# A spiking recommender on one core: the padding row is taken out by a matrix product instead of by masks

## The chip, the cores and the metric

The kernel runs on one core of one Trainium2 chip. The metric is the device time of one execution in microseconds (us); lower is better. Before the change it is 1647.34 us, the median of three runs.

## The reference

For 1024 sequences of 50 items the reference looks up a row of 128 values for each item in a table of 100001 rows, forms a running mean, normalizes it over the batch, drives a leaky spiking neuron with it, and multiplies the mean spike of each sequence with the whole table. Row 0 of the table stands for padding and counts as zero.

```python
emb = emb_table.at[0].set(0.0)                    # 100001 x 128
e = emb[seq]                                      # 1024 x 50 x 128
prefix = jnp.cumsum(e, axis=1)
denom = jnp.minimum(t_idx[None, :], lengths[:, None])   # t_idx = 1..50
uF = prefix / denom[:, :, None]
mean, var = uF.mean(axis=0), uF.var(axis=0)       # over the batch
y = (uF - mean) * lax.rsqrt(var + BN_EPS) * gamma + beta
def step(v, x):                                   # x: y of one time step
    v = v + (x - v) / TAU                         # TAU = 2
    spike = (v - V_TH >= 0)                       # V_TH = 1
    return v - spike * V_TH, spike
_, spikes = lax.scan(step, v0, x_seq)
scores = spikes.mean(axis=0) @ emb.T              # 1024 x 100001, float32
```

The result is 409.6 MB.

## The kernel before

The kernel has two parts with a seam. The order of all instructions on each engine is the order of the program text (`tc.manual_schedule()`): nothing is reordered by a planner. Tiles with the same tag share a place, and an instruction that writes a tile waits for the last readers of what lay there.

**First part: 50 steps, one for each position t.** The layout is transposed: 128 features on the partitions, the 1024 sequences in the free dimension. For each step GpSimd issues 8 indirect DMAs (`gather`, L204), each of which brings the table rows of 128 sequences into one 128x128 piece of the tile `e`. The tile has two buffers. `gather(t + 2)` stands inside step t, and its first DMA has to wait until TensorE has read `e` of step t. `idx` holds the item numbers; the first two tiles are gathered ahead of the loop.

The table's row 0 isn't zero in memory. ScalarE therefore multiplies each gathered piece by `some`, which is 1 where the index is above 0 and 0 elsewhere (`masked`, L249): 8 instructions a step, four ahead of `over` (L254) and four behind it, at the end of step t for the tile of step t + 1.

TensorE transposes the 8 pieces (L296) and adds them into two PSUM tiles `pre[0]` and `pre[1]`, one for each half of the batch, which thereby hold the running sum. Ahead of the loop a product of zeros (L275) opens the two sums. For each half, VectorE divides by the length or the step (`uF`, L307) and takes the statistics (`bs`, L308). Then, for the whole step: the aggregate (`mv`, L312), the square root on ScalarE (`r`, L316), the centring of `uF` on ScalarE (L323), on VectorE the rest of the potential after the spike (`rest`, which writes `negv`, L258), a reciprocal and three tiny operations for the scale `a` (L329 to L342), the input `x` on ScalarE into the tile of `v` (L346), the count of the spikes of the step before (`spiked`, L261), and the new potential `v` (`step`, L349). ScalarE then writes `d`, which is v minus the threshold (`over`, L254). `rest` needs `d`. `v` lies in two PSUM tiles, `v0` and `v1`, by turns.

In two late steps (t = 42 and 44) the first two 1024-item tiles of the table are prepared for the second part (`prepare`): 8 transposes (L135) into a PSUM tile `pt`, a copy, and a subtraction (L152), so that a tile is held as a high and a low part.

The last step is split. Its potential is made in three pieces of the batch: `pieceA` (128 sequences), `pieceB` (512) and `pieceC` (384), so that the products for the first 128 sequences can begin before the others are done. `near` holds what the first piece needs of the old potential, and `vA` and `countA` finish that piece. `keep_busy` (L270) issues transposes whose result nobody reads, 12 between the last real ones and 16 on `near` ahead of the first products.

**Second part: the products.** For each tile of 1024 items and each of the 8 blocks of 128 sequences TensorE multiplies the counts with the high and the low part (L159), VectorE (L476) and ScalarE (L478) by turns scale the result out of PSUM, and SP stores it.

**Setup.** SP loads `idx`, `len_i`, `gb` (gamma and beta), and then the first tiles of the table (`rows`); VectorE computes `some` (L216), the reciprocal lengths `rl`, their broadcast `rb` (L221), and `rlen` after 8 transposes of `rb` (L224), and clears `negv` (L240) and `count`. `rb` and every `uF` share one place.

The pieces of the code that the prediction follows:

Of the kernel before, what the change touches and what calls it, by code (L numbers as in the profile page):

```python
# [12 lines left out]
F32 = mybir.dt.float32  # L13
BF16 = mybir.dt.bfloat16
F32R = mybir.dt.float32r
I32 = mybir.dt.int32
U32 = mybir.dt.uint32
AF = mybir.ActivationFunctionType
ALU = mybir.AluOpType

P = 128
BN_EPS = 1e-5
V_TH = 1.0
HALF = 1024
KQ = HALF // P
BANK = 512
GROUP = 6
AHEAD = 6
TWICE = 2
ASIDE = 2  # L30
SHIFT = TWICE + ASIDE
# [7 lines left out]
def rec_kernel(  # L39
# [9 lines left out]
    nc = tc.nc  # L49
    B, T = seq.shape  # L50
    N, D = table.shape
# [119 lines left out]
    with ExitStack() as ph:  # L171
# [9 lines left out]
        nc.sync.dma_start(out=idx, in_=seq.rearrange("(p n) t -> p n t", n=NB))  # L181
        len_i = once.tile([P, NB], I32, tag="len_i", name="len_i")
        nc.sync.dma_start(out=len_i, in_=lengths.rearrange("(p n) -> p n", n=NB))
        gb = once.tile([P, 2], F32, tag="gb", name="gb")
        nc.sync.dma_start(out=gb[:, 0:1], in_=gamma.rearrange("(d o) -> d o", o=1))
        nc.sync.dma_start(out=gb[:, 1:2], in_=beta.rearrange("(d o) -> d o", o=1))
# [14 lines left out]
        def gather(t):  # L201
            es[t] = gp.tile([P, B], F32, tag="e", name=f"e_{t}")
            for n in range(NB):
                nc.gpsimd.indirect_dma_start(  # L204
                    out=es[t][:, n * P : (n + 1) * P],
                    out_offset=None,
                    in_=table,
                    in_offset=bass.IndirectOffsetOnAxis(ap=idx[:, n, t : t + 1].bitcast(U32), axis=0),
                )

        make_identity(nc, ident)
        rb = up.tile([P, NB, P], F32, tag="uF", name="rb")
        gather(0)

        some = once.tile([P, NB, T], F32, tag="some", name="some")
        nc.vector.tensor_single_scalar(some, idx, 0.0, ALU.is_gt)  # L216

        rl = once.tile([P, NB], F32, tag="rl", name="rl")
        nc.vector.tensor_copy(rl, len_i)
# [7 lines left out]

        hgb = once.tile([P, 3], F32, tag="hgb", name="hgb")
        nc.vector.tensor_scalar_mul(hgb[:, 0:1], gb[:, 0:1], 0.25)
        nc.vector.tensor_scalar_mul(hgb[:, 2:3], gb[:, 0:1], -0.25)  # L230
        nc.vector.tensor_scalar_mul(hgb[:, 1:2], gb[:, 1:2], 0.5)
        eps = once.tile([P, 1], F32, tag="eps", name="eps")
        nc.vector.memset(eps, BN_EPS)
        less = once.tile([P, 1], F32, tag="less", name="less")
# [7 lines left out]

        pre = [accp.tile([P, BANK], F32, tag=f"pre{h}", name=f"pre{h}") for h in range(B // BANK)]

        def masked(t, ns):

            for n in ns:
                part = es[t][:, n * P : (n + 1) * P]
                nc.scalar.activation(part, part, AF.Identity, scale=some[:, n, t : t + 1])  # L249

        def over(t, v):

            d = lp.tile([P, B], BF16, tag="d", name=f"d_{t}")
            nc.scalar.activation(d, v, AF.Identity, bias=less)  # L254
            return d

        def rest(d, v, cs):
            nc.vector.scalar_tensor_tensor(negv[:, cs], d[:, cs], 0.0, v[:, cs], ALU.is_ge, ALU.subtract)  # L258

        def spiked(out, cs, v):  # L260
            nc.vector.scalar_tensor_tensor(out, v, V_TH, count[:, cs], ALU.is_ge, ALU.add)  # L261
# [9 lines left out]

        v = None

        for h in range(B // BANK):
            nc.tensor.matmul(  # L275
                pre[h],
                lhsT=count[:, :P],
                rhs=count[:, h * BANK : (h + 1) * BANK],
                start=True,
                stop=False,  # L280
                skip_group_check=True,
            )
        masked(0, range(NB))
        gather(1)
        for t in range(T):
            last = t == T - 1
            e = es.pop(t)
            if last:
                rest(d, v, pieceA)
                near = once.tile([P, P], F32, tag="r0", name="near")  # L290
                nc.vector.tensor_scalar(near, negv[:, :P], -0.5, hgb[:, 1:2], ALU.mult, ALU.add)
            uF = up.tile([P, B], F32, tag="uF", name=f"uF_{t}")
            bs = sp.tile([P, B // BANK, 6], F32, tag="bs", name=f"bs_{t}")
            for h, cs in enumerate(halves):
                for k in range(0, BANK, P):
                    nc.tensor.matmul(  # L296
                        pre[h][:, k : k + P],
                        lhsT=e[:, h * BANK + k : h * BANK + k + P],
                        rhs=ident,
                        start=False,  # L300
                        stop=last,
                        is_transpose=True,
                        skip_group_check=True,
                    )
                    if last and h and k + P < BANK:
                        keep_busy(ident, KQ // 2)
                nc.vector.scalar_tensor_tensor(uF[:, cs], rlen[:, cs], 1.0 / (t + 1), pre[h], ALU.max, ALU.mult)  # L307
                nc.vector.bn_stats(bs[:, h, :], uF[:, cs])  # L308
            if t + 2 < T:
                gather(t + 2)  # L310
            mv = sp.tile([P, 2], F32, tag="mv", name=f"mv_{t}")
            nc.vector.bn_aggr(mv, bs.rearrange("p h s -> p (h s)"))  # L312


            r = sp.tile([P, 1], F32, tag="r", name=f"r_{t}")
            nc.scalar.activation(r, mv[:, 1:2], AF.Sqrt, bias=eps)  # L316
            if last:
                centred = once.tile([P, P], F32, tag="r0hi", name="centred")
                nc.vector.tensor_scalar(centred, uF[:, :P], mv[:, 0:1], hgb[:, 2:3], ALU.subtract, ALU.mult)
                w = sp.tile([P, 1], F32, tag="w", name="w")  # L320
                nc.vector.tensor_scalar_add(w, mv[:, 1:2], BN_EPS)
            else:
                nc.scalar.activation(uF, uF, AF.Identity, bias=mv[:, 0:1], scale=-1.0)  # L323


            if t and not last:
                rest(d, v, whole)

            nc.vector.reciprocal(r, r)  # L329
            q = sp.tile([P, 1], F32, tag="q", name=f"q_{t}")  # L330
            a = sp.tile([P, 1], F32, tag="a", name=f"a_{t}")
            if last:
                nc.vector.tensor_scalar(q, w, r, r, ALU.mult, ALU.mult)
                nc.vector.scalar_tensor_tensor(q, q, 3.0, r, ALU.subtract, ALU.mult)
                vA = once.tile([P, P], F32, tag="r0n", name="vA")
                nc.vector.scalar_tensor_tensor(vA, centred, q, near, ALU.mult, ALU.add)
                spiked(countA, slice(0, P), vA)
                nc.vector.tensor_mul(a, q, hgb[:, 0:1])
            else:
                nc.vector.scalar_tensor_tensor(q, mv[:, 1:2], BN_EPS, r, ALU.add, ALU.mult)  # L340
                nc.vector.tensor_scalar(q, q, r, 3.0, ALU.mult, ALU.subtract)
                nc.vector.tensor_scalar(a, q, r, hgb[:, 0:1], ALU.mult, ALU.mult)  # L342


            def x(vt, cs):
                nc.scalar.activation(vt, uF[:, cs], AF.Identity, bias=hgb[:, 1:2], scale=a)  # L346

            def step(vt, cs):
                nc.vector.scalar_tensor_tensor(vt, negv[:, cs], -0.5, vt, ALU.mult, ALU.add)  # L349

            if not last:
                vt = vp.tile([P, B], F32, tag=f"v{t % 2}", name=f"v_{t}")
                x(vt, whole)
                if t:
                    spiked(count, whole, v)
                step(vt, whole)
                v = vt
                if t == T - 2:
                    spiked(count, whole, v)
                masked(t + 1, range(NB // 2))  # L360
                d = over(t, v)
                if t in (T - 8, T - 6):
                    q = (t - T + 8) // 2
                    pair(q)
                    prepare(q, vp.tile([P, HALF], F32, tag="v1", name=f"pt_{q}"))
                    if q == TWICE - 1:
                        for k in range(TWICE):
                            rows[GROUP + ASIDE + k] = first[:, k, :]
                        nc.sync.dma_start(
                            out=first[:, :TWICE, :],  # L370
                            in_=table[(GROUP + ASIDE) * HALF : (GROUP + SHIFT) * HALF, :].rearrange(
                                "(q p k) d -> p q (k d)", p=P, k=KQ
                            ),
                        )

                masked(t + 1, range(NB // 2, NB))


        keep_busy(near, 2 * KQ)
# [1 line left out]
            nc.scalar.activation(uF[:, cs], uF[:, cs], AF.Identity, bias=mv[:, 0:1], scale=-1.0)  # L381

        po0 = accp.tile([P, HALF], F32, tag="po0", name="po_0_0")
        po1 = vp.tile([P, HALF], F32, tag="v1", name="po_0_1")
        o0 = gp.tile([P, HALF], F32, tag="e", name="o_0_0")
        o1 = gp.tile([P, HALF], F32, tag="e", name="o_0_1")
        firsts = [(q, po, o, h, cs) for q, po, o in ((0, po0, o0), (1, po1, o1)) for h, cs in enumerate(halves)]
# [14 lines left out]
        rest(d, v, pieceC)  # L402
        for f in firsts:
            first_store(*f)
        vC = vp.tile([P, B - BANK - P], F32, tag="v0", name="vC")
        x(vC, pieceC)
        step(vC, pieceC)
        spiked(countC, pieceC, vC)
# [109 lines left out]
```

## Time and profile before

| | before |
|---|---|
| three runs | 1647.17, 1647.34, 1648.22 us |
| median | 1647.34 us |
| the profiled execution: own time | 1647.17 us |
| its span in the profile | 1645.4 us |
| granted TensorE clock, mean | 0.96 |
| first part, to the last step's square root | 583.5 us |
| from there to the end | 1061.9 us |
| busy in the span: TensorE, VectorE, ScalarE, GpSimd | 63%, 57%, 48%, 23% |
| DMA engines in the second part | 98% busy |

The span runs from the first to the last instruction that the profiler recorded; the execution's own time is 1.77 us longer. Busy shares are means over two parts with different limits: GpSimd, for instance, is busy only while the steps run, at about 0.7 of the time, and idle afterwards. In a row of a timeline the columns are the start, the duration, the engine, the line of the program, the operation, and in brackets the idle time of that engine just before, with what ended it. A group's row gives the busy time and the mean of one instruction in ns, then the idle time ahead of the group's instructions and what ended most of it.

### The profile page before, as it was taken

How to read it: one execution, taken by the hardware profiler on the slowest of the kernel's cores; microseconds unless marked ns; L12 is line 12 of the kernel's file. 1: busy time of each engine (PE TensorE's matmuls, PEld its weight loads, DVE VectorE, ACT ScalarE, POOL GpSimd, SP SyncE). 2: the span in 40 equal slices, each digit the busy share in tenths (PEclk: the TensorE clock that was granted, in tenths of full speed). 3: DMA queues.
4: the chain of work that ended last, by engine and by line, in shares of the span. 5: the costliest groups of instructions: out<-in, count | busy, mean ns of one | idle time of the engine just before them, and what ended most of it. 6: DMA issues, size and time to landing. Idle time of an engine off the chain costs nothing.

```text
span 1645.4 us, 12553 instructions
## 1 busy us (share of the span) xinstructions
PE 1034.7 (63%) x4358; PEld 778.3 (47%) x4358; DVE 945.4 (57%) x1112; ACT 791.6 (48%) x1095; POOL 379.4 (23%) x406
## 2 busy tenths in 40 slices
PE   3222222222222289889998888888888888788884
PEld 1111111111111177667776666666666666666663
DVE  4656666666665765666655555555545555455642
ACT  4455555554554555555644444444444444444442
POOL 7666666666666500000000000000000000000000
PEclk9999999999999999999998999899999999999998
DMA  9611111111111169999999999999999999999998
GB/s 354 227 46 45 46 46 47 50 46 46 49 45 59 50 279 413 409 421 412 404 428 429 429 424 423 416 432 417 408 430 425 427 422 406 430 423 419 426 401 356
DMA packets 51171, 488.06 MB, mean 297 GB/s; under 512 B 10063, under 2 KB 10192, under 8 KB 29860
## 3 DMA queue, kind: packets, MB, share of 16 engines
q1 hardware_dynamic: 30608, 430.80, 62.2%
q0 software_dynamic: 12800, 26.24, 5.4%
q10 hardware_dynamic: 7700, 30.23, 4.5%
q8 instruction: 34, 0.56, 0.1%
q14 instruction: 29, 0.24, 0.0%
HBM read 77.62 MB, written 409.60 MB: 296 GB/s over the span
## 4 chain that ended last, share of the span: by engine, by line
DMA 42%; DVE 17%; PE 17%; ACT 10%; issue 7%; another core or an unknown queue 6%; POOL 0%; ACTq 0%; SPq 0%; DVEq 0%
DMA scores<-o 41%; PE po L159 13%; PE pre L296 3%; DVE bs L308 3%; DVE o L476 3%; DVE uF L307 3%; ACT o L478 3%; DVE negv L258 2%; ACT e L249 2%; ACT d L254 2%; DVE v L349 2%; ACT v L346 1%; ACT uF L323 1%; DVE pairs L152 1%
## 5 line engine op out<-in xcount | busy, mean ns | idle before, releaser
L476 DVE TENSOR_SCALAR o<-po 128x1024 f32<-128x1024 f32 (+1 forms) x391 | 467.8, 1214 | 324.7 <-DMA scores<-o 177.7
L478 ACT ACTIVATE o<-po 128x1024 f32<-128x1024 f32 x391 | 392.2, 1026 | 499.2 <-DMA scores<-o 352.6
L204 POOL DMA_INDIRECT e<-in_L_rec_emb_table,idx x400 | 378.7, 947 | 187.5 <-issue 107.7
L296 PE MATMUL pre<-ident,e 128*128 128x128 f32 x400 | 138.4, 474 | 412.0 <-ACT e L249 208.2
L159 PE MATMUL po<-pairs,countB 128*128 128x512 f32 (+1 forms) x1120 | 291.4, 407 | 57.4 <-ACT o L478 57.4
L296 PEld LDWEIGHTS pre<-ident,e 128*128 128x128 f32 x400 | 73.3, 183 | 477.0 <-ACT e L249 224.1
L159 PE MATMUL po<-pairs,countC 128*128 128x512 f32 (+1 forms) x840 | 239.0, 431 | 56.5 <-ACT o L478 49.0
L159 PEld LDWEIGHTS po<-pairs,countB 128*128 128x128 f32 x1120 | 211.4, 194 | 117.8 <-ACT o L478 75.2
L159 PEld LDWEIGHTS po<-pairs,countC 128*128 128x128 f32 x840 | 167.7, 207 | 108.5 <-ACT o L478 61.1
L307 DVE SCALAR_TENSOR_TENSOR uF<-rlen,pre 128x512 f32<-128x512 f32 x100 | 68.7, 687 | 186.4 <-remote 95.9
L152 DVE TENSOR_TENSOR pairs<-pt,pairs 128x1024 fp32r<-128x1024 f32 x70 | 85.3, 1218 | 95.3 <-ACT pairs L151 95.2
L249 ACT ACTIVATE e<-e,some 128x128 f32<-128x128 f32 x400 | 127.3, 388 | 6.3 <-DMA e<-in_L_rec_emb_table,idx 6.1
L316 ACT ACTIVATE r<-mv,eps 128x1 f32<-128x1 f32 x50 | 14.7, 295 | 222.2 <-DVE mv L312 122.4
L135 PE MATMUL pt<-ident,rows 128*128 128x128 f32 (+1 forms) x768 | 105.2, 282 | 18.1 <-issue 11.5
L135 PEld LDWEIGHTS pt<-ident,rows 128*128 128x128 f32 (+1 forms) x768 | 94.9, 148 | 35.2 <-issue 18.8
L159 PE MATMUL po<-hi,countB 128*128 128x512 f32 x208 | 85.7, 412 | 12.5 <-ACT o L478 12.2
L151 ACT CAST pairs<-pt 128x1024 fp32r<-128x1024 f32 x70 | 70.1, 1013 | 41.5 <-PE pt L135 41.5
L159 PE MATMUL po<-lo,countB 128*128 128x512 f32 x208 | 83.5, 401 | 0.0
L159 PE MATMUL po<-hi,countC 128*128 128x512 f32 x156 | 68.5, 439 | 16.2 <-ACT o L478 15.2
L346 ACT ACTIVATE v<-uF,hgb,a 128x1024 f32<-128x1024 f32 x49 | 59.2, 1207 | 30.9 <-DVE a L342 15.3
L308 DVE BATCH_NORM_STATS2 bs<-uF 128x6 f32<-128x512 f32 x100 | 69.4, 694 | 3.4
L159 PE MATMUL po<-pairs,countA 128*128 128x512 f32 x280 | 68.6, 394 | 4.0 <-ACT o L478 3.4
(79 smaller groups left out, 795.0 us busy)
## 6 DMA issues: line engine op xcount, KB each, us to landing
scores<-o SPq DMA_DIRECT2D x96, 3072.0 KB
scores<-o SPq DMA_DIRECT2D x32, 1536.0 KB
scores<-o SPq DMA_DIRECT2D x30, 1024.0 KB
rows<-in_L_rec_emb_table ACTq DMA_DIRECT2D x19, 1536.0 KB
scores<-o SPq DMA_DIRECT2D x8, 2896.5 KB
rows<-in_L_rec_emb_table SPq DMA_DIRECT2D x5, 3072.0 KB
e<-in_L_rec_emb_table,idx POOLq DMA_INDIRECT x400
rows<-in_L_rec_emb_table SPq DMA_DIRECT2D x2, 1024.0 KB
```

The lines of the kernel that those rows point to most:

```text
L135: nc.tensor.transpose(pt[:, k0 : k0 + pw], r[:pw, k0 : k0 + D], ident[:pw, :pw])
L151: nc.scalar.copy(vh, vp)
L152: nc.vector.tensor_tensor(vl, vp, vh.bitcast(F32), ALU.subtract)
L159: nc.tensor.matmul(po[:, :kw], lhsT=counts[n], rhs=part[:, k0 : k0 + kw], start=j == 0, stop=j == 1,)
L204: nc.gpsimd.indirect_dma_start(out=es[t][:, n * P : (n + 1) * P], out_offset=None, in_=table, in_offset=bass.IndirectOffsetOnAxis(ap=idx[: ...
L249: nc.scalar.activation(part, part, AF.Identity, scale=some[:, n, t : t + 1])
L296: nc.tensor.matmul(pre[h][:, k : k + P], lhsT=e[:, h * BANK + k : h * BANK + k + P], rhs=ident, start=False, stop=last, is_transpose=True, ...
L307: nc.vector.scalar_tensor_tensor(uF[:, cs], rlen[:, cs], 1.0 / (t + 1), pre[h], ALU.max, ALU.mult)
L308: nc.vector.bn_stats(bs[:, h, :], uF[:, cs])
L346: nc.scalar.activation(vt, uF[:, cs], AF.Identity, bias=hgb[:, 1:2], scale=a)
L476: nc.vector.tensor_scalar_mul(o[:, h0 : h0 + hw], po[:, :hw], 1.0 / T)
L478: nc.scalar.mul(o[:, h0 : h0 + hw], po[:, :hw], 1.0 / T)
```

## The change

1. The masks go. The gathered pieces are transposed into `pre` as they are, row 0 included.
2. In their place `correct(t, l)` adds to each half of `pre` a product of 128x128 by 128x512, which takes row 0 out again. Its right side `zT`, built once, has a one at row t for each sequence whose index at step t is 0 (and again at row t + 64). Its left side `l` has, in row t, minus the high part of the table's row 0, and in row t + 64 minus what is left of it. The two products for step t + 1 stand in step t, behind `gather(t + 2)`; those of step 0 also open the sums, in place of the product of zeros.
3. The left sides are written by `only`, one VectorE product of 128x640 for five steps at a time, into a tile `ls`.
4. The setup loads row 0, spread over the partitions (`r0`), builds `isz` (a memset and two comparisons, in place of `some`), turns it by 8 transposes into `zps`, copies that to `zT` and row 0 to `r0hi` on ScalarE, and makes `r0n` and `sel` on VectorE.
5. In the last step, `rest` on the first piece and `near` give way to `moved` and `near`, which are computed straight from `v` after the 49th step. The first piece's quantities are thereby times -2 (`hgb[:, 2:3]` is 0.5 gamma, and the spike's comparison is `<= -2`).
6. The two tiles of `v` change places with the step's parity, and with them those of `pt`, `po1` and `vC`.

```diff
+        r0 = once.tile([P, D], F32, tag="r0", name="r0")
+        nc.sync.dma_start(out=r0, in_=table[0:1, :].to_broadcast([P, D]))
...
+        isz = up.tile([P, NB, P], F32, tag="uF", name="isz")
...
-        some = once.tile([P, NB, T], F32, tag="some", name="some")
-        nc.vector.tensor_single_scalar(some, idx, 0.0, ALU.is_gt)
+        nc.vector.memset(isz, 0.0)
+        for u in (0, P // 2):
+            nc.vector.tensor_single_scalar(isz[:, :, u : u + T], idx, 0.0, ALU.is_equal)
+        zps = vp.tile([P, B], F32, tag="v1", name="zps")
+        for n in range(NB):
+            nc.tensor.transpose(zps[:, n * P : (n + 1) * P], isz[:, n, :], ident)
+        zT = once.tile([P, B], F32R, tag="zT", name="zT")
+        nc.scalar.copy(zT, zps)
+        r0hi = once.tile([P, D], F32R, tag="r0hi", name="r0hi")
+        nc.scalar.copy(r0hi, r0)
+        r0n = once.tile([P, D], F32, tag="r0n", name="r0n")
+        nc.vector.tensor_scalar_mul(r0n, r0hi.bitcast(F32), -1.0)
+        up2 = slice(P // 2, P)
+        nc.vector.tensor_tensor(r0n[up2, :], r0hi[up2, :].bitcast(F32), r0[up2, :], ALU.subtract)
+        sel = once.tile([P, P // 2], F32, tag="sel", name="sel")
+        nc.vector.tensor_tensor(sel, ident[:, : P // 2], ident[:, P // 2 :], ALU.add)
...
-        nc.vector.tensor_scalar_mul(hgb[:, 2:3], gb[:, 0:1], -0.25)
+        nc.vector.tensor_scalar_mul(hgb[:, 2:3], gb[:, 0:1], 0.5)
...
+        beta2 = gb[:, 1:2]
...
-        def masked(t, ns):
-
-            for n in ns:
-                part = es[t][:, n * P : (n + 1) * P]
-                nc.scalar.activation(part, part, AF.Identity, scale=some[:, n, t : t + 1])
+        ls = once.tile([P, ONLY, D], F32R, tag="ls", name="ls")
+
+        def only(t):
+
+            k = t % ONLY
+            if k == 0:
+                n = min(ONLY, T - t)
+                nc.vector.tensor_tensor(
+                    ls[:, :n, :],
+                    r0n.unsqueeze(1).to_broadcast([P, n, D]),
+                    sel[:, t : t + n].unsqueeze(2).to_broadcast([P, n, D]),
+                    ALU.mult,
+                )
+            return ls[:, k, :]
+
+        def correct(t, l):
+            for h in range(B // BANK):
+                nc.tensor.matmul(
+                    pre[h],
+                    lhsT=l,
+                    rhs=zT[:, h * BANK : (h + 1) * BANK],
+                    start=t == 0,
+                    stop=False,
+                    skip_group_check=True,
+                )
...
-        for h in range(B // BANK):
-            nc.tensor.matmul(
...
-        masked(0, range(NB))
+        correct(0, only(0))
+        l = only(1)
         gather(1)
...
-            if last:
-                rest(d, v, pieceA)
-                near = once.tile([P, P], F32, tag="r0", name="near")
-                nc.vector.tensor_scalar(near, negv[:, :P], -0.5, hgb[:, 1:2], ALU.mult, ALU.add)
...
             if t + 2 < T:
                 gather(t + 2)
+            if not last:
+                correct(t + 1, l)
...
-                spiked(countA, slice(0, P), vA)
+                nc.vector.scalar_tensor_tensor(countA, vA, -2.0 * V_TH, count[:, pieceA], ALU.is_le, ALU.add)
...
-                vt = vp.tile([P, B], F32, tag=f"v{t % 2}", name=f"v_{t}")
+                vt = vp.tile([P, B], F32, tag=f"v{(t + 1) % 2}", name=f"v_{t}")
...
-                masked(t + 1, range(NB // 2))
+                    moved = once.tile([P, P], F32, tag="r0hi", name="moved")
+                    nc.vector.tensor_scalar_add(moved, v[:, pieceA], beta2)
+                    near = once.tile([P, P], F32, tag="r0", name="near")
+                    nc.vector.scalar_tensor_tensor(near, v[:, pieceA], V_TH, moved, ALU.is_ge, ALU.subtract)
                 d = over(t, v)
+                if t + 2 < T:
+                    l = only(t + 2)
...
-                    prepare(q, vp.tile([P, HALF], F32, tag="v1", name=f"pt_{q}"))
+                    prepare(q, vp.tile([P, HALF], F32, tag="v0", name=f"pt_{q}"))
...
-                masked(t + 1, range(NB // 2, NB))
...
-        po1 = vp.tile([P, HALF], F32, tag="v1", name="po_0_1")
+        po1 = vp.tile([P, HALF], F32, tag="v0", name="po_0_1")
...
-        vC = vp.tile([P, B - BANK - P], F32, tag="v0", name="vC")
+        vC = vp.tile([P, B - BANK - P], F32, tag="v1", name="vC")
```

In the changed kernel the transposes into `pre` stand at L324, `correct` at L282, `uF` at L335, the aggregate at L342 and the square root at L346.

More of the change, by code (lines that the diff above doesn't have):

```diff
@@ L28 @@
 AHEAD = 6
+ONLY = 5
 TWICE = 2
@@ L272, in rec_kernel @@
         v = None
-        for h in range(B // BANK):
-            nc.tensor.matmul(
[L276 to L282, printed above, removed]
-        masked(0, range(NB))
+        correct(0, only(0))
+        l = only(1)
         gather(1)
```

## The prediction

> **What bounds the kernel now.** I read the page's engine table and its slices first: the recurrence of 50 steps fills the span up to about 584 us, after that VectorE, ScalarE and the stores run to the end at 98% DMA (583.5 to 1645.4, 1061.9 us). The change touches the first part and the seam, so what it is worth is what it takes off those 584 us. Of the costliest groups three matter:
>
> ```profile
> L204 POOL DMA_INDIRECT e<-in_L_rec_emb_table,idx x400 | 378.7, 947 | 187.5 <-issue 107.7
> L307 DVE SCALAR_TENSOR_TENSOR uF<-rlen,pre 128x512 f32<-128x512 f32 x100 | 68.7, 687 | 186.4 <-remote 95.9
> L249 ACT ACTIVATE e<-e,some 128x128 f32<-128x128 f32 x400 | 127.3, 388 | 6.3 <-DMA e<-in_L_rec_emb_table,idx 6.1
> ```
>
> The masks (L249) are the group that goes. That ScalarE is busy with them says nothing yet: does anything wait for them? Next the timeline of ScalarE, where L316 marks each step once (start, duration, idle time before):
>
> ```profile
> 341.71 0.29 ACT L316 ACTIVATE r<-mv,eps 128x1 f32<-128x1 f32 x1 [2.26 <-DVE mv L312]
> 350.72 0.29 ACT L316 ACTIVATE r<-mv,eps 128x1 f32<-128x1 f32 x1 [2.26 <-DVE bs L308]
> 364.55 0.29 ACT L316 ACTIVATE r<-mv,eps 128x1 f32<-128x1 f32 x1 [7.07 <-DVE bs L308]
> 377.97 0.29 ACT L316 ACTIVATE r<-mv,eps 128x1 f32<-128x1 f32 x1 [6.67 <-DVE mv L312]
> 386.99 0.29 ACT L316 ACTIVATE r<-mv,eps 128x1 f32<-128x1 f32 x1 [2.26 <-DVE mv L312]
> ```
>
> Steps of 9.01, 13.83, 13.42 and 9.02 us: two short, two long, 45.28 us for four, and so on from the fifth step to the forty-third. A short step is the arithmetic with the masks in it. The long ones are something else. GpSimd's timeline over the same time, only the rows after a pause:
>
> ```profile
> 331.24 0.95 POOL L204 DMA_INDIRECT e<-in_L_rec_emb_table,idx  x1 [4.45 <-remote]
> ...
> 363.09 0.95 POOL L204 DMA_INDIRECT e<-in_L_rec_emb_table,idx  x1 [2.14 <-remote]
> ...
> 376.52 0.94 POOL L204 DMA_INDIRECT e<-in_L_rec_emb_table,idx  x1 [3.72 <-remote]
> ```
>
> All other gathers follow at 1.2525 us (0.95 and 0.30 of issue). 32 of them are 40.08 us; the two pauses add 1.83 and 3.41 beyond the usual 0.31: 45.3. So GpSimd's gathers and its pauses make the four steps, not the masks. It pauses because the first gather of step t+2 waits for TensorE's transposes of step t, and these end late:
>
> ```profile
> 356.65 1.35 PE L296 MATMUL pre<-ident,e 128*128 128x128 f32 x4 [1.02 <-ACT e L249]
> ```
> ```profile
> 362.85 0.69 DVE L307 SCALAR_TENSOR_TENSOR uF<-rlen,pre 128x512 f32<-128x512 f32 x1 [5.77 <-remote]
> ```
>
> The four transposes start by 357.5, their masks done, but VectorE, which waits for nothing else, is let go at 362.8. TensorE's semaphore events in between lie 2.1 and 2.8 us apart. Where this starts is regular: after GpSimd resumes at 331.2, 514.9 and 537.8 some 20 transposes end on time (steps of 8, and 8 more for each extra tile at L135), whether that takes 26, 16 or 27 us. Once gathers have paused for over 3 us, several completions come at once. I read it as a store of completions that fills while gathers run and empties when they stop; what it is, the trace doesn't say.
>
> **The change, part by part.** *Masks out.* 8 ScalarE instructions a step go, four of them between the step's end and its transposes. In a short step VectorE waits 0.51 and 0.95 us for the transposes (L307); with them early those go, and the arithmetic shrinks from 9.01 to about 7.55 us. Both lie under 8 x 1.2525 = 10.02 us of gathers. Taken alone the masks' end is worth nothing in the loop.
>
> *Two products of 128x512 a step in* (`correct`): TensorE executes 10 matmuls a step for 8. Their busy time (L275's pair took 1.03 us) lies in TensorE's idle time, 10.82 busy of 45.27. They wait for `uF` of the step before, and the next transposes are queued behind them; who waits for those is the next `uF`, at least 4 us later. What they do cost is room in that store. By matmuls, 20 are reached after 2.0 steps, before after 2.5; by instructions (weight load, matmul, and the two separate semaphore waits a step that go) 18 a step become 20: 45 are reached after 2.25. Either way TensorE falls behind in the third step after a pause, the gathers run into it at the third's end, and the pause must be a long one, since after the short one (1.83) the lateness went on. Three steps then take 30.06 + 3.41 = 33.5 us, 11.16 a step against 11.32. Over the 46 steps from the third on: **-7.4 us**. The bounds from the same rows: four steps with the long pause alone, (40.08 + 3.41)/4 = 10.87, -20.7 us; three steps with both pauses, (30.06 + 5.24)/3 = 11.77, +20.7 us. I take the middle one, since the trace shows long pauses that clear the store and none shorter.
>
> [...]
>
> *`only`*: a VectorE product of 128x640 every fifth step, by L152's 128x680 row (0.86 us) some 0.8 us each. VectorE is busy 28.55 of 45.27 us; it lies in the wait before `uF` and costs nothing; without that cover 10 x 0.8 = 8 us. It waits for the fifth `correct` to have read `ls`; `uF` is queued behind it, and waits for later transposes of the same queue anyway.
>
> *Setup.* SP issues one more DMA (0.43 us by its neighbours), ahead of `gb` and the `rows`, which are needed at 7.7 us and 500 us. VectorE gets a memset (0.91 by L240), two comparisons (0.37 each by L216), and waits for 8 more transposes (1.94 by L224), as `rb` takes `isz`'s place; then `only`. ScalarE's copies lie beside. VectorE, done with setup at 9.6, is done near 15.6; the second half of the first step waits for gathered rows until 19.3, and that hides it. If it didn't, 1.8 us, as the first half would start at 15.6 for 13.84. But GpSimd: its first gather took 1.29 us for 0.95 while VectorE copied `rb` (0.69 us). The 1.65 us of new work on SBUF beside gathers costs by that row 0 to 0.8 us; I take **+0.3**. [...]
>
> *Last step.* `rest` and `near` at its start become `moved` and `near` right after the 49th step, no longer behind `d` on ScalarE, and the masks of the last `e` are gone. Before, from one L316 to the next it took 12.60 us (570.92 to 583.52), VectorE being done with the 49th step's count at 576.63, while the second half's masks came only here:
>
> ```profile
> 576.66 1.11 ACT L254 ACTIVATE d<-v,less 128x1024 bf16<-128x1024 f32 x1 [1.35 <-DVE count L261]
> 577.67 1.27 ACT L249 ACTIVATE e<-e,some 128x128 f32<-128x128 f32 x4
> ```
>
> Now: 576.63, `moved` and `near` 0.64, two `uF` and two `bn_stats` 2.76 with gaps, the aggregate 0.24: L316 at 580.3, **-3.2 us** (0 if the transposes are late). The 12 warming transposes run earlier, and their 16 fellows on `near` end some 2 us ahead of the first product, where before they ended 1.7 ahead, at the full clock (spacing 0.213 us until 582.0, then 0.109). If the clock is low, 8 products lose about 0.2 us each: 0 to +1.6, I take **+0.7**. The first piece's spike from `near` has as many operations as before: 0.
>
> *The tiles of v*: `zps` takes v1 before `rps` takes v0, and names swap with parity, so the third piece is still in the tile that held the last v: 0.
>
> Sum: -7.4 + 0.3 - 3.2 + 0.7 = -9.6. The profiled execution's own time is 1647.17 (span 1645.4 and 1.77 around it), the lowest of three and 0.17 under the median. Forecast: 1637.6 us.
>
> **The rivals.** *Slower: the store decides.* The two products fill it faster than pauses empty it, so three steps need both pauses: 11.77 a step, +20.7 - 2.2 = +18.5, 1665.7 us. It decides from 3.9 us of pauses in three steps on (11.32 x 3 - 30.06). For it: two matmuls more in eight. Against: transposes now start as rows land, so TensorE has longer to catch up.
> *The lateness goes.* If ScalarE's 8 instructions on `e` feed the same store, gathers run unbroken: 46 x 1.30 = 60 us less, with the seam 1585. For it: in some long steps the masks too end 0.7 us late; against: they are on time when it starts.
> *Nothing moves in the loop*: pauses shift but keep 5.2 us for four steps; the seam's 2.2 remain: 1645.
>
> **How the numbers follow.** Forecast (three- or four-step cycles with one long pause, 1623 to 1645) 0.5; slower 0.25; lateness gone 0.1; nothing 0.15. Measurement tells 0.2% (3.3 us) from no change. Faster: 0.9 of the first, the third, a fifth of the last: 0.58. Slower: 0.25 and 0.02. Same: 0.15. The range runs from 1620 (the four-step bound with the seam) to 1667 (the slower rival with the unknown costs); it leaves out the unbroken gathers and worse than both pauses.
>
> **What would show it.** Right: L324 transposes start without ScalarE, short steps near 7.6 us, GpSimd pauses once in three steps for 3 us or more, 11.0 to 11.2 us a step on average, the last step 9.4. Wrong: gathers with no pause at all, an average step over 11.3, `uF` waiting for `only`, or a first step later than 21.3 us at L316.

## The result, and the profile after

The changed kernel takes 1638.68 us (median of 14 runs, 1637.18 to 1646.72), the kernel before 1648.02 in the runs beside it: a ratio of 0.9949, 95% interval [0.9939, 0.9960]. The forecast was 1637.6. The profiled execution has 1638.64 us of its own time and a span of 1636.8. The groups that answer to those shown of before:

```profile
L207 POOL DMA_INDIRECT e<-in_L_rec_emb_table,idx x400 | 380.4, 951 | 183.5 <-issue 110.9
L335 DVE SCALAR_TENSOR_TENSOR uF<-rlen,pre 128x512 f32<-128x512 f32 x100 | 68.0, 680 | 161.7 <-remote 124.4
L282 PE MATMUL pre<-zT,ls 128*128 128x512 f32 x100 | 78.4, 786 | 271.2 <-DVE uF L335 227.2
```

The masks' 127.3 us of ScalarE are gone, and 78.4 us of products are on TensorE. VectorE's idle time ahead of `uF` fell by only 25 us, and what ends most of it is still "remote": a semaphore event that the profile puts down to no instruction. `uF` waits there for nothing but the transposes, so it is read as a transpose that reports late. The steps, by ScalarE's square root:

```profile
378.50 0.29 ACT L346 ACTIVATE r<-mv,eps 128x1 f32<-128x1 f32 x1 [16.78 <-DVE mv L342]
385.84 0.29 ACT L346 ACTIVATE r<-mv,eps 128x1 f32<-128x1 f32 x1 [1.76 <-DVE bs L336]
393.25 0.30 ACT L346 ACTIVATE r<-mv,eps 128x1 f32<-128x1 f32 x1 [1.76 <-DVE mv L342]
402.69 0.29 ACT L346 ACTIVATE r<-mv,eps 128x1 f32<-128x1 f32 x1 [3.85 <-DVE bs L336]
423.73 0.30 ACT L346 ACTIVATE r<-mv,eps 128x1 f32<-128x1 f32 x1 [15.45 <-DVE mv L342]
```

A short step is now 7.35 us (9.02 before), a long one 21. Together the four take 45.23 us, for 45.28 before. GpSimd's timeline says why, the rows after a pause:

```profile
331.83 0.94 POOL L207 DMA_INDIRECT e<-in_L_rec_emb_table,idx  x1 [5.38 <-PE pre L282]
...
377.04 0.94 POOL L207 DMA_INDIRECT e<-in_L_rec_emb_table,idx  x1 [5.42 <-remote]
...
422.27 0.94 POOL L207 DMA_INDIRECT e<-in_L_rec_emb_table,idx  x1 [5.56 <-remote]
```

One pause of 5.1 beyond the usual 0.3, behind 32 gathers, where there were two of 1.83 and 3.41. (Most cycles of this trace are like that; one, at 272 and 287, still has two pauses, and one pause, at 94, comes behind 24.) The loop as such is no faster: 45.2 / 4 = 11.30 us a step for 11.32.

So where did 8.6 us of span go? Between marks of the two profiled executions (the last gather starts at 566.60 and 564.20, the last two square roots at 570.92 and 583.52, then 564.70 and 573.90):

| stretch | before | after | difference |
|---|---|---|---|
| start to the last gather | 566.60 | 564.20 | -2.4 |
| last gather to the 49th step's root | 4.32 | 0.50 | -3.8 |
| the last step, root to root | 12.60 | 9.20 | -3.4 |
| root to the end | 1061.9 | 1062.9 | +1.0 |

The first row contains pauses that are shorter by 4.0 us in sum (59.8 for 63.8), hold-ups of single gathers that are longer by 2.6, a first gather that starts 0.15 later, and about 1.1 us of pace: from one start to the next it is 0.003 us less. The second is the end of the loop: before, the 49th step's transposes came in only as the gathers ended; after, they are done as the last gather starts. How the second and the third row share their gain changes from trace to trace (see `last-undone` below); their sum is 7.2 us here, and 8.9 in the two later traces of the changed kernel.

### The profile page after: what moved, and what is told of

It is laid out like the page before. It is cut to its first block, busy times and chain, and to the rows that moved or that the text cites. A ratio compares the mean times of both kernels' runs of the same rounds, so it can differ in the third digit from the quotient of the medians.

```text
span 1636.8 us, 12254 instructions
## 1 busy us (share of the span) xinstructions
PE 1085.8 (66%) x4464; PEld 806.9 (49%) x4464; DVE 948.7 (58%) x1127; ACT 673.0 (41%) x697; POOL 381.1 (23%) x406
## 4 chain that ended last, share of the span: by engine, by line
DMA 42%; PE 16%; DVE 14%; another core or an unknown queue 9%; POOL 7%; issue 5%; ACT 5%; ACTq 0%; SPq 0%; DVEq 0%; POOLq 0%
DMA scores<-o 40%; PE po L160 14%; POOL e L207 7%; DVE o L512 3%; ACT o L514 3%; DVE uF L335 2%; DVE bs L336 2%; DMA e<-in_L_rec_emb_table,idx 2%; DVE v L379 2%; DVE negv L298 1%; ACT v L376 1%; PE pre L324 1%; DVE count L301 1%; DVE pairs L153 1%
## 5 line engine op out<-in xcount | busy, mean ns | idle before, releaser
L282 PE MATMUL pre<-zT,ls 128*128 128x512 f32 x100 | 78.4, 786 | 271.2 <-DVE uF L335 227.2
L282 PEld LDWEIGHTS pre<-zT,ls 128*128 128x128 f32 x100 | 29.0, 291 | 309.9 <-DVE uF L335 255.7
L324 PE MATMUL pre<-ident,e 128*128 128x128 f32 x400 | 126.8, 435 | 79.5 <-DMA e<-in_L_rec_emb_table,idx 63.0
L335 DVE SCALAR_TENSOR_TENSOR uF<-rlen,pre 128x512 f32<-128x512 f32 x100 | 68.0, 680 | 161.7 <-remote 124.4
L324 PEld LDWEIGHTS pre<-ident,e 128*128 128x128 f32 x400 | 80.4, 209 | 126.8 <-DMA e<-in_L_rec_emb_table,idx 94.7
L346 ACT ACTIVATE r<-mv,eps 128x1 f32<-128x1 f32 x50 | 14.8, 295 | 273.0 <-DVE mv L342 181.0
L294 ACT ACTIVATE d<-v,less 128x1024 bf16<-128x1024 f32 x49 | 54.5, 1113 | 65.4 <-DVE v L379 36.3
```

Source lines behind the costliest of these rows:

```text
L282: nc.tensor.matmul(pre[h], lhsT=l, rhs=zT[:, h * BANK : (h + 1) * BANK], start=t == 0, stop=False, skip_group_check=True,)
L324: nc.tensor.matmul(pre[h][:, k : k + P], lhsT=e[:, h * BANK + k : h * BANK + k + P], rhs=ident, start=False, stop=last, is_transpose=True, ...
```

## The experiments

Each kernel ran beside the kernel before on the same chip. The chip wasn't always the same one, and that turned out to be the first finding.

**The two parts alone.** `none` leaves out the pair of products behind `gather(t + 2)`:

```diff
-            if not last:
-                correct(t + 1, l)
```

> The changed kernel without the products in the loop: correct runs for step 0 alone, so row 0 stays in the sums of the later steps. It is the end of the masks alone. Theory A (a store that each TensorE instruction fills and a pause of the gathers empties): 16 TensorE instructions a step for 20, so the pause of 5.1 us comes once in five steps for four: (50.1 + 5.1) / 5 = 11.04 us a step for 11.30, 46 steps, -12 us: 1627 us. Theory B (the pause follows the gathers, once in 32, whatever TensorE does, as the traces of both kernels have it): 1639 us, four steps of 45.2 us.

`double` has the line `correct(t + 1, l)` twice; `narrow` cuts it to 128 columns; `both` puts two products of zeros into the kernel before.

> The changed kernel with both products of each step issued twice (row 0 is taken out twice). Theory A: 24 TensorE instructions a step, a pause of 5.1 us once in three steps: (30.06 + 5.1) / 3 = 11.72 us a step, 46 x 0.42 = +19 us: 1658 us. Theory B: 1639 us, four steps of 45.2 us.

> The changed kernel with the products of the loop 128 columns wide for 512, as many of them: row 0 is taken out of a quarter of the batch. Theory A, by instructions: no change, 1639 us, one pause in four steps. If it is TensorE's working time or its traffic that fills the store: a quarter of it, so near the kernel without products: 1627 us. Theory B: 1639 us.

> The kernel before, masks and all, with two products of zeros of 128x512 into the sums in the place of correct. It is the products alone. Theory A: 20 TensorE instructions a step and the two separate waits, once in three steps the pauses of 5.2 us: (30.06 + 5.2) / 3 = 11.75 us a step for 11.32, +20 us: 1668 us. Theory B: 1648 us.

| chip | before | none | narrow | double | both |
|---|---|---|---|---|---|
| 9 | 1573.44 | 1572.69, 0.9995 [0.9986, 1.0005] | 1572.83, 0.9998 [0.9989, 1.0008] | 1571.89, 0.9991 [0.9981, 1.0000] | 1575.72, 1.0013 [1.0004, 1.0023] |
| 6 | 1573.38 | 1572.51, 0.9995 [0.9986, 1.0005] | | 1572.21, 0.9993 [0.9983, 1.0002] | 1575.18, 1.0012 [1.0002, 1.0022] |

Neither theory, since the base had moved: the kernel before takes 74 us less on these two chips. The trace of `none` shows the difference, first GpSimd's line of the slices, then the steps:

```profile
POOL 7777777777776000000000000000000000000000
```
```profile
318.37 0.29 ACT L344 ACTIVATE r<-mv,eps 128x1 f32<-128x1 f32 x1 [4.33 <-DVE mv L340]
328.49 0.29 ACT L344 ACTIVATE r<-mv,eps 128x1 f32<-128x1 f32 x1 [4.53 <-DVE mv L340]
338.43 0.30 ACT L344 ACTIVATE r<-mv,eps 128x1 f32<-128x1 f32 x1 [4.35 <-DVE mv L340]
348.35 0.30 ACT L344 ACTIVATE r<-mv,eps 128x1 f32<-128x1 f32 x1 [4.33 <-DVE mv L340]
```

GpSimd never pauses, and all steps take 10.0 us, 8 gathers of 1.25. Without late completions (so I call the transposes that are read as reporting late) the loop is bound by the gathers, 10.0 us a step; masks out, no products, one quarter or twice of them differ by less than 0.2% there. That is the prediction's "taken alone the masks' end is worth nothing in the loop", measured where the gathers are unbroken; with late completions the masks' end without the products was run only as the first stretch of `stages` below. `both` is 2.3 us slower than before at unbroken gathers. Its last root lies where that of `none` does (509.3 and 509.2), so the loss comes behind it; the products of the last step's second piece start 0.3 us later against the root than in the others, which doesn't explain it all, and I leave it open.

Three of them ran again, meant for a chip with late completions; it was chip 6 (second row of the table), another without:

> The changed kernel without the products in the loop again (row 0 stays in the sums of steps after the first), for a chip where before takes some 1648 us; where it takes 1573, it repeats the first experiment. Theory A, store filled by TensorE's instructions: 16 a step for 20, 80 a cycle are reached in five steps: pauses of 5.1 us behind every 40 gathers, not 32: 46 / 5 x 5.1 = 47 us of pauses for 61: 1640 - 13 = 1627 us. Theory B, 32 gathers a cycle whatever TensorE does: 1640 us.

> The changed kernel with both products of each step twice (row 0 is taken out twice), for a chip where before takes some 1648 us. Theory A: 24 TensorE instructions a step, 80 a cycle are reached within the fourth step, so a pause of 5.1 us behind every 24 gathers: 46 / 3 x 5.1 = 78 us of pauses for 61: 1640 + 17 = 1657 us. Theory B: 1640 us, pauses behind every 32 gathers.

> The kernel before, masks and all, with two products of zeros a step, for a chip where before takes some 1648 us. Theory A: two more TensorE matmuls a step with the masks' later start: both pauses (5.2 us) in three steps for four: 46 / 3 x 5.2 = 80 us of pauses for 64: 1648 + 16 = 1664 us. Theory B: 1648 us and the pauses behind 8 and 24 gathers by turns as before. A third way, in which the masks' late start is what made two pauses of one: 1648 us too, but no single pauses of 5 us.

The times repeat those of chip 9 within 0.6 us.

**The change again, and its last step undone.** `last-undone` puts `rest` and `near` back to the head of the last step:

```diff
-                    moved = once.tile([P, P], F32, tag="r0hi", name="moved")
-                    nc.vector.tensor_scalar_add(moved, v[:, pieceA], beta2)
...
+            if last:
+                rest(d, v, pieceA)
```

> The changed kernel itself, beside the kernel before on the same chip. If TensorE's late completions belong to the program, before is near 1648 us and this near 1639. If they belong to the chip or to the profiler's state there, as the 1573.4 us of before in the first four experiments suggest, before is near 1573 us with unbroken gathers, and then only the seam and the hold-ups of GpSimd are left of the change: last gather 2.0 us later (503.69 to 501.69 in the runs with and without only), the last step some 3 us shorter: -1 us, 1572 us, no change that can be measured.

> The changed kernel with the last step's first piece as before: rest on the first piece and near at the head of the last step, behind d on ScalarE, and no moved. If the last step's gain came from moved and near: 3.2 us slower than the changed kernel. If it came from the masks, which are gone here too, and moved and near only save the wait for d: before, uF started 1.70 us behind the 49th step's count, the changed kernel takes 0.64 for moved and near, so 1.1 us slower than the changed kernel.

On chip 0 before took 1649.03, the changed kernel 1640.30 (0.9951 [0.9935, 0.9968]), `last-undone` 1640.23 (0.9946 [0.9929, 0.9963]). As times they are equal, with four runs each that spread over 1.8 and 4.6 us, more than what is sought. The trace of `last-undone`:

```profile
570.52 1.22 DVE L301 SCALAR_TENSOR_TENSOR count<-v,count 128x1024 bf16<-128x1024 f32 x1
572.92 0.29 DVE L298 SCALAR_TENSOR_TENSOR negv<-d,v 128x128 f32<-128x128 bf16 x1 [1.18 <-ACT d L294]
573.25 0.29 DVE L323 TENSOR_SCALAR near<-negv,hgb 128x128 f32<-128x128 f32 x1
573.45 0.68 DVE L339 SCALAR_TENSOR_TENSOR uF<-rlen,pre 128x512 f32<-128x512 f32 x1
```

VectorE waits 1.18 us for `d`; from the count's end to `uF` 1.71 us. In the first trace of the changed kernel:

```profile
569.17 1.22 DVE L301 SCALAR_TENSOR_TENSOR count<-v,count 128x1024 bf16<-128x1024 f32 x1
570.32 0.34 DVE L391 TENSOR_SCALAR moved<-v,gb 128x128 f32<-128x128 f32 x1
570.69 0.29 DVE L393 SCALAR_TENSOR_TENSOR near<-v,moved 128x128 f32<-128x128 f32 x1
570.90 0.68 DVE L335 SCALAR_TENSOR_TENSOR uF<-rlen,pre 128x512 f32<-128x512 f32 x1
```

0.51 us. The last step is 10.41 us in `last-undone` and 9.20 here, so by these two traces `moved` and `near` are worth 1.2 of the 3.4 us and the masks' end the other 2.2, as the second expectation has it. The other two traces of the changed kernel don't repeat it. In `after-again`, which ran beside `last-undone`:

```profile
567.16 0.29 DVE L393 SCALAR_TENSOR_TENSOR near<-v,moved 128x128 f32<-128x128 f32 x1
570.03 0.69 DVE L335 SCALAR_TENSOR_TENSOR uF<-rlen,pre 128x512 f32<-128x512 f32 x1 [2.57 <-remote]
```

The 49th step's root comes at 561.17 there, 3.8 us before the last gather starts; then the last step's transposes report late, `uF` waits for them and not for `near`, and the last step takes 11.87 us, as in `after-third`. From the last gather's start to the last root it is 16.92 us before, 11.61 in `last-undone`, and 9.70, 8.06 and 8.05 in the three traces of the changed kernel. So the gain at the loop's end is there in all of them, most of it without `moved` and `near`; what those two are worth in time isn't shown.

**Stretches in one kernel.** One kernel has three stretches, `(0 if 1 <= t < 14 else 2 if 14 <= t < 28 else 1)` pairs a step and then four more buffers:

```diff
+            k = t % 6 - 2
+            if k >= 0 and 28 <= t < T - 9:
+                es[t] = embp.tile([P, B], F32, tag=("hi1", "lo1", "hi0", "lo0")[k], name=f"e_{t}")
+            else:
...
-                correct(t + 1, l)
+                for _ in range(0 if 1 <= t < 14 else 2 if 14 <= t < 28 else 1):
+                    correct(t + 1, l)
```

> The changed kernel in stretches, to be read by GpSimd's pauses in each: steps 1 to 13 without the products, steps 14 to 27 with each pair twice, steps 28 to 40 with one pair and six buffers for the gathered tiles instead of two (the added four in the places of the first tiles' high and low parts, which are free until step 42). Row 0 stays in the sums of the first stretch and is taken out twice in the second. On a chip with late completions, theory A (TensorE's instructions fill the store): a pause of 5 us behind 40 gathers in the first stretch, behind 24 in the second; theory B: behind 32 in both. In the third, if a pause is what empties the store and the buffers only let the gathers run on, the pauses come behind some 64 gathers, of at least the same 5 us; if a pause comes by itself after 32 gathers, behind 32 as now. On a chip without them: no pauses, and all stretches take 8 x 1.25 = 10.0 us a step.

> The changed kernel itself, once more. On a chip where before takes 1648 us: 1640. On a chip where it takes 1573: GpSimd's gathers are unbroken, only holds them up by 2.0 us, the end of the loop is bound by the last gathers' landing; the kernels with none and with twice the products took 1572.5 and 1572.0 there, so this one 1572.3: 1.1 us less than before, within 0.2%.

Chip 2 has late completions: before 1647.80, the changed kernel 1641.09 (0.9962 [0.9948, 0.9976]), `stages` 1656.59 (1.0054 [1.0033, 1.0074]). GpSimd's rows after a pause, all three stretches:

```profile
70.90 0.95 POOL L211 DMA_INDIRECT e<-in_L_rec_emb_table,idx  x1 [5.46 <-remote]
103.33 0.95 POOL L211 DMA_INDIRECT e<-in_L_rec_emb_table,idx  x1 [2.71 <-remote]
116.69 0.95 POOL L211 DMA_INDIRECT e<-in_L_rec_emb_table,idx  x1 [3.67 <-remote]
171.22 0.95 POOL L211 DMA_INDIRECT e<-in_L_rec_emb_table,idx  x1 [4.55 <-remote]
...
184.70 0.95 POOL L211 DMA_INDIRECT e<-in_L_rec_emb_table,idx  x1 [3.52 <-remote]
...
230.09 0.95 POOL L211 DMA_INDIRECT e<-in_L_rec_emb_table,idx  x1 [3.80 <-remote]
264.10 0.95 POOL L211 DMA_INDIRECT e<-in_L_rec_emb_table,idx  x1 [4.14 <-remote]
297.37 0.94 POOL L211 DMA_INDIRECT e<-in_L_rec_emb_table,idx  x1 [3.54 <-remote]
```
```profile
353.09 0.95 POOL L211 DMA_INDIRECT e<-in_L_rec_emb_table,idx  x1 [5.99 <-remote]
...
410.69 0.95 POOL L211 DMA_INDIRECT e<-in_L_rec_emb_table,idx  x1 [7.17 <-PE pre L286]
...
455.98 0.94 POOL L211 DMA_INDIRECT e<-in_L_rec_emb_table,idx  x1 [5.57 <-PE pre L286]
...
508.76 0.95 POOL L211 DMA_INDIRECT e<-in_L_rec_emb_table,idx  x1 [22.43 <-PE pre L328]
```

Without products the pauses lie 32 and then 40 gathers apart (70.9, 103 and 117, 171); with twice the products, from 230 on, 24 apart. That is the way theory A has it, but thin: the step from 32 to 40 came once only, and a pause behind 24 comes singly in the changed kernel too (at 94.34 in its first trace). Firmer is that in the profiles of both kernels one pause near the loop's end follows the one before it after only 16 gathers (514.86 and 537.83 before, 512.84 and 535.48 after), where the second table tile's 8 extra transposes stand. The length of a pause seems to move with it: 3.2 to 3.8 us beyond the usual behind 24 in this stretch, about 5.1 behind 32 in the changed kernel, though its single pause behind 24 is 4.5. From the pause at 70.9 to that at 171.2 a step takes 11.15 us, from 184.7 to 297.4 it takes 11.27, and the changed kernel's 11.30. With so few pauses the cut matters: 70.9 to 184.7 gives 11.38. So within what one run can tell the sum is nearly the same whatever TensorE does, and theory B's time comes out of theory A's pauses.

The third stretch refutes what I had built on A. With six buffers the pauses come behind 40, 40, 32 and 24 gathers, not 64, and when two buffers return GpSimd waits 22 us: from 297.4 to 508.8, a span that begins with twice the products, 8 gathers take 12.4 us on average. I read it so that while GpSimd runs on, TensorE only falls further behind. More buffers didn't remove the pauses; by this reading they are when TensorE catches up.

**What held the gathers up.** The last kernel takes VectorE's work out of GpSimd's way: ScalarE makes `ls`, and `negv` and `count` are cleared ahead of the first gather.

```diff
-                nc.vector.tensor_tensor(
-                    ls[:, :n, :],
-                    r0n.unsqueeze(1).to_broadcast([P, n, D]),
-                    sel[:, t : t + n].unsqueeze(2).to_broadcast([P, n, D]),
-                    ALU.mult,
-                )
+                for u in range(n):
+                    nc.scalar.activation(ls[:, u, :], r0n, AF.Identity, scale=sel[:, t + u : t + u + 1])
```

> The changed kernel with the work taken off VectorE that stood in GpSimd's way in the traces: the left sides ls made by ScalarE, 128x128 at a time, five at a time as before, and negv and count cleared at the very start, ahead of the first gather. If a VectorE operation on SBUF that begins first holds the gather that begins inside it: no gather over 1.2 us but the first (for 2.3 us of the ninth and 1.1 to 1.5 of those behind ls), the last gather 2.0 us earlier; where gathers are unbroken that is 1570.3 us for the 1572.3 between the kernels with none and twice the products, where TensorE's completions are late some 1638 for 1640, less sure, since the pauses fall otherwise. If the hold-ups are hidden: 1572.3 or 1640.

On chip 8, where before takes 1644.65 us: 1633.79, a ratio of 0.9936 [0.9922, 0.9949]. That is a little better than the changed kernel's 0.9949, 0.9951 and 0.9962, with intervals that overlap; they weren't run side by side. No gather but the first takes over 0.95 us. Pauses are mostly 32 apart still:

```profile
352.19 0.94 POOL L207 DMA_INDIRECT e<-in_L_rec_emb_table,idx  x1 [5.28 <-remote]
```

Counted from the first gather, its last one starts 2.7 us earlier than in the profile of the changed kernel (558.1 for 560.8), the sum of the pauses being the same (59.8 us each): the hold-ups' 2.6 us, against the 2.0 expected. A step of the loop takes 11.25 us.

## Why the prediction was right, and where not

The time was right, and so was the way of reading the kernel before: gathers and late transposes make the loop, not the masks. That the sum came out was luck: up to the last gather 2.4 us were gained where the prediction had 7.1, and 3.8 us that weren't in the sum, at the loop's end, made up for it. Point by point:

- **Masks out, "worth nothing in the loop"**: right, as far as it was run. `none` is 0.9995 of before where completions aren't late; the short step fell to 7.35 us (forecast 7.55), and four steps still take 45.2.
- **The loop's -7.4**: the step that failed. Three-step cycles with one long pause (11.16 a step) didn't come; there are four-step cycles with one pause of 5.1, 11.30 a step, 0.9 us less over 46 steps. The error was to take the pause of 3.41 as the length that empties the store, whatever led up to it. `stages` shows three-step cycles with pauses of 3.2 to 3.8, but with twice the products. What made the sum come out is the end: -3.8 us, as the 49th step no longer waits for the gathers to end, which I had not costed, with pauses shorter by 4.0 from the start to the last gather. In three traces of the changed kernel the last root lies 8.1 to 9.7 us behind the last gather's start, before 16.9. That gain is real, but no cycle gave it. Of the signs that the prediction named, the short step (7.35 us for 7.6) and, in one trace, the last step (9.2 for 9.4) came; the average step did not: 11.30 us is its bound for being wrong.
- **"`only` costs nothing", and +0.3 for the setup**: failed. I asked whether VectorE has time for it, not whether a gather takes longer beside it. It cost GpSimd 2.6 us:

```profile
13.61 2.32 POOL L207 DMA_INDIRECT e<-in_L_rec_emb_table,idx  x1 [0.30 <-issue]
...
65.85 1.19 POOL L207 DMA_INDIRECT e<-in_L_rec_emb_table,idx  x1 [0.30 <-issue]
```
```profile
13.53 0.91 DVE L260 MEMSET negv<- 128x1024 f32 x1 [0.16 <-issue]
14.36 0.76 DVE L272 TENSOR_TENSOR ls<-r0n,sel 128x640 fp32r<-128x640 f32 x1
...
65.41 0.82 DVE L272 TENSOR_TENSOR ls<-r0n,sel 128x640 fp32r<-128x640 f32 x1
```

  The work that the prediction priced for the setup, a memset and two comparisons for `isz`, shows no loss against before: the first gather, which begins inside the comparisons, takes 1.16 us for 1.29. The gather at 65.85 begins inside `ls` and ends 0.81 us after it; that at 13.61 begins inside the memset of `negv` and ends 0.81 after `ls`. Before, the same memset began 0.07 us after its gather and held nothing (0.95). The gathers that had begun 0.04, 0.08 and 0.30 us before an `ls` weren't held (0.94); the other five that began inside an `ls` took 0.97 to 1.43 us and ended 0.81 us after it too. The copy of `rb` (0.69 us), by which the prediction priced the setup, lies across a gather of 0.94 here. But it began 0.03 us after that gather, and an `ls` that begins after its gather holds none either. A copy from SBUF that begins first did not occur; that of `rlen`, out of PSUM, did (11.40 to 12.63), and the gather at 12.36 took 0.94. The setup's share is 1.26 us (0.22 and 1.38 for 0.34), beyond my bound of 0.8.
- **Last step -3.2**: right in the profile of the result, -3.4, 9.20 for 9.4. In the two later traces the step takes 11.87 us, -0.7: the prediction's own "0 if the transposes are late". There the 49th step had come sooner, 3.8 us before the last gather starts for 0.5 behind it. The split into 1.2 for `near` and 2.2 for the masks rests on one trace of each kernel.
- **Seam +0.7, "if the clock is low"**: in the profile of the result it is zero. The granted clock is 0.94 from 574 to 580, and the products follow each other at 0.23 us. `after-again`, with 0.50 from 572.8 to 579.3, shows the other case:

```profile
574.90 0.77 PE L160 MATMUL po<-hi,countA 128*128 128x512 f32 x1 [4.43 <-DVE a L368]
575.46 0.63 PE L160 MATMUL po<-lo,countA 128*128 128x512 f32 x1
575.89 0.63 PE L160 MATMUL po<-hi,countA 128*128 128x512 f32 x1
576.31 0.63 PE L160 MATMUL po<-lo,countA 128*128 128x512 f32 x1
```

  At 0.43 us apart, ten products lose 0.2 each: 16 evictions later the second part is 1.4 us behind, 18.77 for 17.37 us after the root. Two of the changed kernel's three traces have it, within the bound of 1.6; but from the root to the end they take 1065.0 and 1063.7 us, +3.1 and +1.8, so not all of it is the products. The +1.0 of the profile shown is not in these products: its first 16 evictions end 17.4 us after the root for 17.3 before. It arises later. The cause of the rest stays open.
- **The tiles of `v`, 0**: nothing in the traces speaks against it; it wasn't tried alone.
- **The rivals**: "the lateness goes" happened on two of the experiments' five chips, for both kernels alike, so not by the change: `none` and `double` have no pauses there, and `both`, with the masks, has its last root at 509.3. "Nothing moves in the loop" was nearly right about the cycle (5.1 us of pauses in four steps for 5.2) and wrong about the end. "The store decides" didn't come even with twice the products.

What makes completions late stays open, and no run here shows it. The traces show that it comes with gathers under way (in the changed kernel short steps of 7.35 us follow a pause, then a long one of 21), and the times that it belongs to the chip or its state: the same kernel takes 1573 us on chips 6 and 9 and 1645 to 1649 on 0, 2 and 8. That it depends on how many instructions TensorE issues is likely, from the spacing of the pauses in `stages` (32 and 40 gathers without the products, 24 with twice of them).

## What to carry to other kernels

Ask of an operation that is moved onto an idle engine whether another engine's instructions take longer beside it (gathers that began inside `ls` or the memset took 0.97 to 2.32 us for 0.94), not only whether the engine has time. Where the chain is a bound that gives way and returns (pauses that empty something), don't price one cycle with the pause of another: measure how the pause grows with what led up to it. And look at the last two rounds of a loop by themselves, since what hides the arithmetic in the middle is gone there; here 7 of the 9 us came from them, and how they are shared between the two changes from run to run.

## What the runs showed of the hardware that was not expected

- One kernel, 1573 us on two chips and 1645 to 1649 on others, most of it in pauses of one loop (63.8 us in the profile before): a comparison that isn't made on one chip can be off by 4.7%.
- The granted clock halved without effect on the loop. In the profiled execution after it was 0.50 through the loop, before 1.00:

```profile
100.00:200.00 100.00, 35.59 (x91) 19.38 (x91) 67.17 (x114) 34.01 (x37) 67.84 (x73) 0.50 0.16 47
```
```profile
100.00:200.00 100.00, 22.92 (x66) 11.98 (x66) 62.95 (x107) 50.49 (x99) 65.20 (x70) 1.00 0.16 46
```

  The columns are the stretch, then busy time and instructions of TensorE, its weight loads, VectorE, ScalarE and GpSimd, the granted clock, the DMA share and GB/s. Transposes that wait for no input lie 0.21 us apart at either clock (eight at 378.14 take 1.91 us after, four at 507.30 take 1.06 before). `after-again` had 1.00 there, and its four steps take the same 45.2 us. Behind the root it was otherwise: the products lay 0.43 us apart at 0.50. Runs of the changed kernel with a mean clock of 0.79 to 0.80 (1637.95, 1638.43, 1638.64, 1646.72) spread like those at 0.94 to 0.96 (1637.18 to 1644.67).
- Six buffers for two went with a slower loop, 12.4 us a step for 11.3, where completions are late. It is one stretch of one run, and it includes the 22 us as two buffers return.
